# Merging three matrix products of a slot, splitting a norm over slots, and taking square roots on another engine

## The chip, the cores and the metric

The kernel runs on one core of a Trainium2 chip. A core has a matrix engine (TensorE, PE in the profile, with PEld for its weight loads), a vector engine (VectorE, DVE), an engine for activation functions (ScalarE, ACT), a general engine (GpSimd, POOL) and an engine that issues DMAs (SyncE, SP). Each works through its own queue in order; they wait for each other through semaphores. The metric is the time of one execution in microseconds (us); lower is better. Before the change it was 1166.24 us, the median of three runs (1165.88 to 1167.61).

## What is computed

The reference is a small perceiver of two layers over 64 batches of 32 latent rows of 256 features, so 2048 rows:

```
x = x + L0_xattn(layernorm(x), ctx)      # cross attention
x = x + L0_attn(layernorm(x))            # self attention, changed here
x = x + L0_ffn(layernorm(x))             # 16 blocks, the best 4 per row
x = x + L1_xattn(...); x = x + L1_attn(...); x = x + L1_ffn(...)
```

The self attention of layer 0 norms its input a second time, makes 16 heads of queries of 128 features, and one key and one value that all heads share:

```
xn = layernorm(x) * g_norm
q = xn @ Wq                    # 16 heads x 128
k, v = split(xn @ Wkv)         # one head
q, k = l2norm(q), l2norm(k)    # times 4 each
attn = softmax(q @ k.T)        # over the 32 rows of a batch
out = layernorm((attn @ v) @ Wout) * g_out
```

The feed forward part behind it chooses 4 of 16 blocks for each row by a softmax over a small product (`Wr`), and multiplies the hidden values with the mask of the chosen blocks.

## The kernel before

All 2048 rows lie in SBUF as 16 tiles `xs[t]` of 128 rows (4 batches each); four tiles make a group `g`. The self attention is a loop over slots, `for t in range(NT + 1)` with NT = 16. In its pool the order of the work on PE, DVE, ACT and POOL is the order in which the program is written (`manual_schedule`), so each engine's queue can be read off the code. Work of tile t and tile t-1 is interleaved in slot t:

- `query_part(n)` (line 868): two of the 16 heads of queries for a pair of tiles, a product `qb`, copied out by ACT (876). It runs ten parts ahead, one in each of the places 0 to 3 of a slot.
- `similar(t)`: scores `Sb` (899), four products that each use 32 columns of TensorE, one for each batch; then the sums of the squared queries `ssb` (907), of the same form. ACT takes the square root `rqb` (916).
- `gather(t - 1)`: the contexts `avb` of the tile before (946), four products that each use 32 rows of TensorE. DVE copies two of them into `oTb` (951), ACT the other two (953).
- `scale(t)`: DVE's reciprocal of `rqb` (921) and the product with the scores (923). `power(t)`: the exponential on ACT (927).
- `square(t + 1)`: POOL squares the next tile's queries (887).
- `project(t - 1)`: 16 products `yb` with the output weights (959). `norm_stats` and `norm_out`: the norm of the result, with ACT's square root (971), DVE's `ynb` (983) and POOL's product and addition to `xs[t]` (984, 985).
- `share(t)`: the denominators `denb` (933), their reciprocal (935) and the product (936), which gives the weights that the next slot's `gather` reads.
- `rotate(t)` and `fetch(t + 1)`: POOL's preparation of the context for layer 1, with its DMAs on SP, and `write_pad(t)`, which clears a tile on DVE (135, 136) and sends it out.

Into these slots other work is placed by `at(slot, place, function)`; `place(z)` issues query part z (for z below 4) and then what was placed there, in the order of the `at` calls. The places that matter here:

- keys of group g: `keys_norm(g)` (the two norms in a row, with statistics on DVE, lines 172 and 173, and ACT's square roots, 163) in slot 3 for group 2 and slot 6 for group 3, place 5; `keys_turn` (transposes and copies) in slots 4 and 8, place 2; `keys_of` (products `kvp`, 364, copies and squares on ACT, scaling on DVE, 378 to 380) in slots 5 and 9, places 1 and 3; `turn_keys` (transposes `kTp`, 387, copied by DVE, 389) in slots 6 and 10, place 2.
- routing of group g: `choose_norm` in slot 4g+5, place 5; `choose_turn` (transposes `tpr`, 633, copied by ACT, 636) in slot 4g+6, place 1; `choose_blocks` and `choose_best` (a product, 646, and then up to 26 small DVE instructions, 653 to 683) in slots 4g+7 and 4g+8, place 5.
- at the end of slot 2 DVE fills some number tables (756 to 764).
- from slot 10 on, the feed forward part of group 0: its norm (`ln_group(0, "c")`, slot 10, place 5), transposes (slot 12), hidden products (slots 13 to 15).

The products of a slot share eight PSUM banks: one for the scores, four (tag `W`) that `ssb`, the denominators and the four `avb` take in turn, one for `yb`, and two (tag `mm`) for everything else. A product that reuses a bank waits until the engine that reads its former content is done. `rstd_of` has two forms: a square root on ACT with a reciprocal on DVE, or, with `power=True`, an addition and a power of -0.5 on POOL (157, 158).

Of the kernel before, what the change touches and what calls it, by code (L numbers as in the profile page):

```python
# [7 lines left out]
F32 = mybir.dt.float32  # L8
AF = mybir.ActivationFunctionType
ALU = mybir.AluOpType  # L10
# [3 lines left out]
P = 128  # L14
B, S, D = 64, 32, 256
NT = B * S // P
# [11 lines left out]
EPS = 1e-5  # L28
# [19 lines left out]
def perceiver_kernel(ctx: ExitStack, tc: tile.TileContext, a: dict, out: bass.AP):  # L48
    nc = tc.nc
# [19 lines left out]
    def sm(name, shape):  # L69
        return small.tile(shape, F32, tag=name.split("_")[0], name=name)  # L70
# [4 lines left out]
    xs = [x[:, :D] for x in xf]  # L75
# [69 lines left out]
    mhalf = const.tile([P, 4], F32, name="mhalf")  # L145
# [62 lines left out]
    def ln_group(g, name, twice=False, act=False, power=False, sign=None):  # L208

        mv = sm(f"lnm_{name}{g}", [P, 4, 2])  # L210
        for i in range(4):
            stats(mv[:, i, :], xs[4 * g + i], f"{name}{g}_{i}", sign)
        rs, sh = ln_scale(mv, f"{name}{g}", twice, power)
        return [ln_out(xs[4 * g + i], rs, sh, i, f"{name}{g}", act) for i in range(4)]
# [127 lines left out]
    latT = {}  # L342
# [6 lines left out]
    def keys_norm(g):  # L349
        latT[g] = ln_group(g, "b", twice=True, act=True, power=g == 0)  # L350
# [273 lines left out]
    def choose_norm(g, act=True):  # L624
        choice[g] = ln_group(g, "r", act=act)

    def choose_turn(g, ps, work):
        xn = choice[g]
        xT = choice[g] = work.tile([P, KC, 512], F32, tag="xTr", name=f"xTr{g}", bufs=1)
        for k in range(KC):  # L630
            tp = ps.tile([P, 512], F32, tag="mm", name=f"tpr{g}_{k}")
            for i in range(4):
                nc.tensor.transpose(
                    tp[:, i * P : (i + 1) * P], xn[i][:, k * P : (k + 1) * P], ident
                )
            nc.scalar.copy(xT[:, k, :], tp)
        return xT
# [198 lines left out]
    with tc.tile_pool(name="wB", bufs=2) as work, tc.tile_pool(  # L836
# [167 lines left out]

        steps = {}

        def at(slot, place, fn):
            steps.setdefault((slot, place), []).append(fn)  # L1010

        for g in range(1, NG):
            at(4 * g - 4, 2, lambda g=g: keys_turn(g, ps2))
            slot, place_ = (0, 5) if g == 1 else (4 * g - 3, 1)
            at(slot, place_, lambda g=g: keys_of(g, ps2, 0))
            at(4 * g - 3, 3, lambda g=g: keys_of(g, ps2, 1))
            at(4 * g - 2, 2, lambda g=g: turn_keys(g, ps2))
            if g > 1:
                at((3, 6)[g - 2], 5, lambda g=g: keys_norm(g))
        for g in range(NG - 1):  # L1020
            at(4 * g + 5, 5, lambda g=g: choose_norm(g))
            at(4 * g + 6, 1, lambda g=g: choose_turn(g, ps2, work))
            at(4 * g + 7, 5, lambda g=g: choose_blocks(g, ps2, work))
            if g < NG - 2:
                at(4 * g + 7, 5, lambda g=g: choose_best(g, work, (0, 1)))
            at(4 * g + 8, 5, lambda g=g: choose_best(g, work, (2, 3)))
            if g < NG - 2:
                at(4 * g + 9, 2, lambda g=g: choose_store(g, ps2, work))
# [24 lines left out]

        at(10, 4, lambda: ff.update(mb=spread(0)))
        at(16, 2, lambda: ff.update(mb1=spread(1)))
        at(10, 5, lambda: ff.update(xn=ln_group(0, "c", act=True)))
        at(12, 2, ff_begin)
        for f, (slot, place) in enumerate(
            ((13, 2), (13, 3), (14, 0), (14, 1), (14, 2), (14, 3), (15, 0), (15, 1))
# [8 lines left out]
        for t in range(NT + 1):  # L1068


            parts = [AHEAD + 4 * t + z for z in range(4)]

            def place(z):
                if z < 4:
                    query_part(parts[z])
                for step in steps.get((t, z), ()):
                    step()

            if t < NT:
                similar(t)  # L1080
            place(0)
            if t > 0:
                gather(t - 1)
            if t < NT:
                scale(t)
            place(1)
            square(t + 1)
            ff_late()
            place(2)
            if t < NT:  # L1090
                power(t)
            ff_late()
            place(5)
            if t > 0:
                project(t - 1)
                norm_stats(t - 1)
            if t < NT:
                share(t)
            place(3)
            ff_late()  # L1100
            if t > 0:
                norm_out(t - 1)
            if t < NT:
                rotate(t, work)
            if t + 1 < NT:
                fetch(t + 1, work)
            place(4)
            if t == 2:
                numbers = all_numbers(counted)
                tri, one, token, base = (numbers[z] for z in ("tri", "one", "token", "base"))  # L1110
                ntile, n128e, n128h = (numbers[z] for z in ("ntile", "n128e", "n128h"))
            if t > 2:
                for t_ in {3: (0, 1), NT: (NT - 2, NT - 1)}.get(t, (t - 2,)):
                    nc.gpsimd.tensor_copy(xf[t_][:, D : D + 1], token[:, t_ : t_ + 1])
            write_pad(t)
            if t in (2, 4):
                load_c(t // 4)
# [1411 lines left out]
```

## Time and profile before

| | |
|---|---|
| median of three runs | 1166.24 us |
| profiled execution, its own time | 1165.13 us |
| its span, first to last instruction | 1163.4 us |
| TensorE's granted clock, mean | 0.988 |
| busy: PE, PEld | 1106.1, 788.6 us |
| busy: DVE, ACT, POOL | 769.4, 579.1, 455.9 us |
| the loop over slots | about 146 to 490 us of the span |

The page gives the busy time of each engine, the span in 40 slices, and the costliest groups of instructions. A line of a timeline gives the start, the length, the engine, the line of the program, the operation, the tile written and the tiles read, the shape and how many instructions were merged; in brackets, for how long the engine was idle before it and which engine ended that. A float32 matrix product counts as two instructions. A line of the table of stretches gives, after the bounds and the length, the busy time (and the number of instructions) of PE, PEld, DVE, ACT and POOL, the granted clock, the busy share of the DMA engines, and GB/s. A line of the list of waits says who waited for whom: the sum, how often, and the longest.

### The profile page before, as it was taken

Reading aid. Unit: us, or ns where it says so; the run is one execution under the profiler, and the core shown is the slowest. Engines: PE = TensorE matmul, PEld = TensorE weight load, DVE = VectorE, ACT = ScalarE, POOL = GpSimd, SP = SyncE. Lnnn points to the kernel's source line nnn. Section 1 sums busy time; section 2 is a strip of 40 time slices with the busy share of each in tenths; the row PEclk is TensorE's granted clock in tenths of the full one; section 3 lists DMA queues with packets and bytes.
Section 4 is the critical chain, followed back from the end, with each engine's and each line's share of the span. In section 5 each row is a group of like instructions: output and inputs, shape, how many; then the busy total and the mean of one; then the engine's idle time right before and its main releaser. Section 6 shows DMA issues by size and latency. Waiting matters only on the chain. (4 is left out here: it accounts for less than half of the span.)

```text
span 1163.4 us, 26376 instructions
## 1 busy us (share of the span) xinstructions
PE 1106.1 (95%) x10026; PEld 788.6 (68%) x10026; DVE 769.4 (66%) x1810; ACT 579.1 (50%) x1446; POOL 455.9 (39%) x766
## 2 busy tenths in 40 slices
PE   8999999899999999999998999999999988889997
PEld 5666766677767657667676777777776656555663
DVE  4886146868987987655225787777878566675532
ACT  3446363545455364231326777777777545442221
POOL 2443265777768787410001121121222356632111
PEclk9999999999999999999999999999999999999999
DMA  5221132546346446491213121212110175112413
GB/s 138 70 77 38 33 87 82 169 124 169 96 129 205 115 121 188 144 281 60 74 47 57 29 55 29 56 28 56 38 46 2 35 223 184 49 34 74 152 37 119
DMA packets 98990, 109.05 MB, mean 94 GB/s; under 512 B 37240, under 2 KB 73465, under 8 KB 98642
## 3 DMA queue, kind: packets, MB, share of 16 engines
q1 hardware_dynamic: 97138, 103.05, 31.2%
q0 software_dynamic: 1728, 4.33, 1.0%
q8 instruction: 80, 1.31, 0.5%
q14 instruction: 44, 0.36, 0.1%
HBM read 76.36 MB, written 31.41 MB: 93 GB/s over the span
## 5 line engine op out<-in xcount | busy, mean ns | idle before, releaser
L1441 ACT ACTIVATE pp<-Sd,nm 128x256 f32<-128x256 f32 x256 | 119.6, 480 | 39.9 <-POOL nm L1438 39.9
L868 PE MATMUL qb<-xT_b,b_q 128*128 128x256 f32 x512 | 122.3, 386 | 0.4 <-ACT qTb L876 0.4
L868 PEld LDWEIGHTS qb<-xT_b,b_q 128*128 128x128 f32 x512 | 94.7, 190 | 39.6 <-issue 19.3
L959 PE MATMUL yb<-b_o,oTb 128*128 128x256 f32 x512 | 115.2, 383 | 0.6 <-DVE oTb L951 0.5
L1437 DVE TENSOR_REDUCE nm<-Sd 128x2 f32<-128x512 f32 x128 | 79.4, 682 | 54.7 <-PE Sd L1424 54.7
L1438 POOL TENSOR_SCALAR nm<-nm 128x2 f32<-128x2 f32 x128 | 26.9, 210 | 222.9 <-DVE nm L1437 222.6
L959 PEld LDWEIGHTS yb<-b_o,oTb 128*128 128x128 f32 x512 | 97.3, 192 | 15.1 <-issue 1.6
L1459 DVE TENSOR_TENSOR pp<-pp,rd 128x512 f32<-128x512 f32 x128 | 89.5, 699 | 4.4
L1475 ACT COPY pTd<-pt 128x512 f32<-128x512 f32 x128 | 68.8, 590 | 10.5 <-PE pt L1469 4.8
L1469 PE MATMUL pt<-cst,pp 128*128 128x128 f32 x512 | 67.9, 274 | 5.9 <-DVE pp L1459 4.9
L887 POOL TENSOR_TENSOR q2b<-qTb 128x512 f32<-128x512 f32 x64 | 64.7, 1041 | 13.9 <-ACT qTb L876 13.9
L1469 PEld LDWEIGHTS pt<-cst,pp 128*128 128x128 f32 x512 | 59.1, 141 | 15.4 <-ACT ld L1449 4.9
L876 ACT COPY qTb<-qb 128x512 f32<-128x512 f32 x64 | 37.3, 584 | 63.7 <-PE qb L868 60.9
L1236 PE MATMUL qd<-xT_d,d_m 128*128 128x256 f32 x256 | 64.1, 394 | 0.7 <-DVE rd L1458 0.3
L921 DVE RECIPROCAL rqb<-rqb 128x512 f32<-128x512 f32 x16 | 53.5, 3342 | 17.1 <-ACT rqb L916 17.1
L1516 PE MATMUL yd<-d_n,co 128*128 128x256 f32 x256 | 63.2, 391 | 0.0
L1424 PE MATMUL Sd<-ct,qTd 64*128 64x256 f32 x480 | 60.0, 388 | 0.0
L1450 POOL TENSOR_TENSOR sd<-sd,ld 128x2 f32<-128x2 f32 x128 | 26.3, 206 | 85.8 <-ACT ld L1449 85.8
L722 PE MATMUL yc<-c,hc 128*128 128x256 f32 x256 | 58.5, 382 | 0.0
L1490 PE MATMUL od<-pTd,na 128*64 128x256 f32 x480 | 58.4, 385 | 0.0
L1516 PEld LDWEIGHTS yd<-d_n,co 128*128 128x128 f32 x256 | 46.2, 189 | 16.7 <-DVE nm L1437 7.7
L935 DVE RECIPROCAL rdb<-denb 128x512 f32<-128x512 f32 x16 | 53.6, 3353 | 5.8 <-PE denb L933 5.6
(424 smaller groups left out, 2417.6 us busy)
## 6 DMA issues: line engine op xcount, KB each, us to landing
srt<-pad SPq DMA_DIRECT2D x17, 1040.0 KB
mb<-maskd SPq DMA_DIRECT2D x64, 128.0 KB
ct<-ctd SPq DMA_DIRECT2D x30, 257.0 KB
rct<-in_ctxT_dram SPq DMA_DIRECT2D x32, 128.5 KB
rrt<-in_ctxT_dram SPq DMA_DIRECT2D x64, 64.2 KB
ctd<-rct SPq DMA_DIRECT2D x32, 128.5 KB
nad<-rna SPq DMA_DIRECT2D x16, 256.0 KB
fw<-in_f_wg_dram SPq DMA_DIRECT2D x16, 256.0 KB
```

Source lines behind the costliest of these rows:

```text
L722: nc.tensor.matmul(y_ps, hs[f][:, i * P : (i + 1) * P], c_2[:, f, :], start=(f == 0), stop=(f == 7),)
L868: nc.tensor.matmul(q_ps[:, hh, :], b_q[:, k, h * P : (h + 1) * P], xT[:, k, c0 : c0 + 256], start=(k == 0), stop=(k == KC - 1),)
L887: nc.gpsimd.tensor_tensor(q2[:, 4 * h4 : 4 * h4 + 4, :], q, q, ALU.mult)
L959: nc.tensor.matmul(y_ps, oT[:, h, :], b_o[:, h, :], start=(h == 0), stop=(h == NH - 1))
L1236: nc.tensor.matmul(q_ps[:, r, :], m[:, k, pr * P : (pr + 1) * P], xT[:, k, c0 : c0 + 256], start=(k == 0), stop=(k == KC - 1),)
L1424: nc.tensor.matmul(logits[b][hh][:, u, :], qT[hs, b % 8, 4 * u : 4 * u + 4, :], ct[hs, b % 4, :KEYS], start=True, stop=True,)
L1437: nc.vector.tensor_reduce(nm, s_ps[hh], AX.X, ALU.max, negate=True)
L1441: nc.scalar.activation(pb[:, u, hh, :], s_ps[hh][:, u, :], AF.Exp, bias=nm[:, u : u + 1], accum_out=sd[:, u : u + 1],)
L1459: nc.vector.tensor_tensor(pp, pp, bc(rd, 2, KEYS), ALU.mult)
L1469: nc.tensor.transpose(pts[c][:, hh * 256 + u * P : hh * 256 + u * P + P], probs[b][:, u, hh, c * P : (c + 1) * P], ident,)
L1475: nc.scalar.copy(pT[:, c, :], pt)
L1516: nc.tensor.matmul(y_ps, co[:, pr, :], n[:, pr, :], start=(pr == pr0), stop=(pr == pr0 + n_pr - 1),)
```

## The change

Three things change in the self attention of layer 0.

In slots 1 to 15 (`inner`), `similar(t)` moves behind `gather(t - 1)`, and query part 1, with what was placed there, moves ahead of `gather`. PE's queue then has two query blocks, the contexts, the scores and the squares in a row, where before it had scores, squares, a query block, contexts and a query block.

The keys' norm of groups 2 and 3 is written out in three steps in three slots (1, 2, 3 and 4, 5, 6): the statistics and a first power, then the second variance and a second power, then the product of the two and the normed rows.

The powers of these norms, of the routing's norms (groups 0 to 2) and of the norm of the feed forward part of group 0 are taken on POOL, with the shift too for the latter two; their normed rows are made on ACT at place 3 of the same slot (place 4 for group 2). The routing's transposes move from place 1 to place 2.

```diff
+        def norm_begin(g, name):
+            mv = sm(f"lnm_{name}{g}", [P, 4, 2])
+            for i in range(4):
+                stats(mv[:, i, :], xs[4 * g + i], f"{name}{g}_{i}")
+            rs = rstd_of(mv, 4, f"{name}{g}", True)
+            sh = sm(f"lnh_{name}{g}", [P, 4])
+            nc.gpsimd.tensor_tensor(sh, rs, mv[:, :, 0], ALU.mult)
+            nc.gpsimd.tensor_scalar(sh, sh, -1.0, None, ALU.mult)
+            begun[name, g] = rs, sh
+
+        def norm_end(g, name):
+            rs, sh = begun.pop((name, g))
+            return [ln_out(xs[4 * g + i], rs, sh, i, f"{name}{g}", True) for i in range(4)]
+
+        def keys_norm_step(g, z):
+            if z == 0:
+                mv = work.tile([P, 4, 2], F32, name=f"kbm_{g}", bufs=1)
+                for i in range(4):
+                    stats(mv[:, i, :], xs[4 * g + i], f"b{g}_{i}")
+                r1 = work.tile([P, 4], F32, name=f"kbr_{g}", bufs=1)
+                nc.gpsimd.tensor_scalar(r1, mv[:, :, 1], EPS, None, ALU.add)
+                nc.gpsimd.tensor_tensor(r1, r1, mhalf[:, 0:4], ALU.pow)
+                begun["b", g] = mv, r1
+            elif z == 1:
+                mv, r1 = begun["b", g]
+                r2 = work.tile([P, 4], F32, name=f"kbq_{g}", bufs=1)
+                nc.vector.tensor_tensor(r2, mv[:, :, 1], r1, ALU.mult)
+                nc.vector.tensor_tensor(r2, r2, r1, ALU.mult)
+                nc.gpsimd.tensor_scalar(r2, r2, EPS, None, ALU.add)
+                nc.gpsimd.tensor_tensor(r2, r2, mhalf[:, 0:4], ALU.pow)
+                begun["b", g] = mv, r1, r2
+            else:
+                mv, r1, r2 = begun.pop(("b", g))
+                nc.vector.tensor_tensor(r2, r2, r1, ALU.mult)
+                nc.vector.scalar_tensor_tensor(r1, mv[:, :, 0], -1.0, r2, ALU.mult, ALU.mult)
+                latT[g] = [ln_out(xs[4 * g + i], r2, r1, i, f"b{g}", True) for i in range(4)]
...
             if g > 1:
-                at((3, 6)[g - 2], 5, lambda g=g: keys_norm(g))
+                for z in range(3):
+                    at((1, 4)[g - 2] + z, 5, lambda g=g, z=z: keys_norm_step(g, z))
         for g in range(NG - 1):
-            at(4 * g + 5, 5, lambda g=g: choose_norm(g))
-            at(4 * g + 6, 1, lambda g=g: choose_turn(g, ps2, work))
+            at(4 * g + 5, 5, lambda g=g: norm_begin(g, "r"))
+            at(4 * g + 5, 3 + g // 2, lambda g=g: choice.update({g: norm_end(g, "r")}))
+            at(4 * g + 6, 2, lambda g=g: choose_turn(g, ps2, work))
...
-        at(10, 5, lambda: ff.update(xn=ln_group(0, "c", act=True)))
+        at(10, 5, lambda: norm_begin(0, "c"))
+        at(10, 3, lambda: ff.update(xn=norm_end(0, "c")))
...
-            if t < NT:
+            inner = 0 < t < NT
+            if t == 0:
                 similar(t)
             place(0)
+            if inner:
+                place(1)
             if t > 0:
                 gather(t - 1)
+            if inner:
+                similar(t)
             if t < NT:
                 scale(t)
-            place(1)
+            if not inner:
+                place(1)
             square(t + 1)
```

More of the change, by code (lines that the diff above doesn't have):

```diff
@@ L1002, in perceiver_kernel @@
                 square(0, (n_ // 2,))
+        begun = {}
+        def norm_begin(g, name):
[32 more added lines that the diff above has]
+                latT[g] = [ln_out(xs[4 * g + i], r2, r1, i, f"b{g}", True) for i in range(4)]
         steps = {}
```

## The prediction

> **What bounds the kernel now.** I read the page first (busy times, slices), then the busy table cut at every context product of layer 0's self attention, then the timelines of PE and DVE in single slots, then PE's list of waits. A slot is one turn of the loop over the 16 tiles; slot 7 is the one whose context product starts at 285.06.
>
> ```profile
> PE 1106.1 (95%) x10026; PEld 788.6 (68%) x10026; DVE 769.4 (66%) x1810; ACT 579.1 (50%) x1446; POOL 455.9 (39%) x766
> ```
>
> PE is the bound over the whole span. What counts in the changed stretch is PE's idle time and what it pays for switching shapes. The next table holds periods from one context product to the next (slots 3, 7, 8, 11, 12, 13); the idle time is the period less PE's busy time:
>
> ```profile
> 202.88:223.85 20.97, 18.30 (x91) 13.02 (x90) 19.89 (x40) 10.12 (x18) 14.84 (x15) 1.00 0.49 133
> 285.06:306.59 21.53, 19.85 (x108) 14.89 (x107) 19.38 (x31) 8.13 (x13) 15.28 (x16) 1.00 0.43 121
> 306.59:326.21 19.62, 19.29 (x98) 13.81 (x98) 18.80 (x27) 8.13 (x12) 15.43 (x16) 1.00 0.40 115
> 368.12:389.21 21.09, 19.85 (x108) 14.89 (x107) 18.82 (x29) 8.12 (x13) 14.84 (x16) 1.00 0.56 165
> 389.21:408.83 19.62, 19.29 (x99) 13.81 (x99) 18.80 (x27) 7.93 (x12) 15.43 (x16) 1.00 0.40 116
> 408.83:428.96 20.13, 18.87 (x84) 11.00 (x83) 17.75 (x30) 14.48 (x20) 16.88 (x18) 1.00 0.45 124
> ```
>
> The reader is to see that in slots 3, 7, 8, 11 and 12 DVE (third figure) is busy 18.8 to 19.9 us: there it is nearly a second bound. PE's list of waits names the same places:
>
> ```profile
> PE avb L946 <- DVE pTb L936: 5.1, 3, 2.2
> PE ssb L907 <- POOL q2b L887: 1.2, 2, 1.0
> PE yb L959 <- DVE oTb L951: 0.5, 1, 0.5
> ```
>
> The 5.1 us are 2.16 at the end of slot 3 (keys' norm of group 2 on DVE), 1.68 after slot 7 and 1.24 after slot 11 (routing choices on DVE). PE's order in an undisturbed slot:
>
> ```profile
> 362.52 1.89 PE L868 MATMUL qb<-xT_b,b_q 128*128 128x256 f32 x8
> 364.34 1.07 PE L899 MATMUL Sb<-qTb,kTb 128*32 128x512 f32 x8
> 365.22 1.04 PE L907 MATMUL ssb<-q2b,ones 128*32 128x512 f32 x8
> 366.19 1.99 PE L868 MATMUL qb<-xT_b,b_q 128*128 128x256 f32 x8
> 368.12 1.14 PE L946 MATMUL avb<-pTb,kvb 32*128 32x512 f32 x8
> 369.19 3.72 PE L868 MATMUL qb<-xT_b,b_q 128*128 128x256 f32 x16
> 372.75 0.52 PE L646 MATMUL lpc<-c_r,xTr 128*128 128x16 f32 x4
> ```
>
> The starts show the price of a switch: a query block between its like takes 1.73 (340.85 to 342.58), before S 1.82, between ss and av 1.93; two of them after av take 3.56, not 3.46; av lasts 1.07 and S 0.88 to the next start.
>
> **The change, part by part.** Sums are made against the profiled execution (span 1163.4, time 1165.13, 1.1 under the median of 1166.24).
>
> *1. One switch a slot.* The seven steps above take 10.23 (362.52 to 372.75). In the new order (q, q, q, av, S, ss, q) they take 1.73+1.73+1.83, then av and S, then 0.97+1.83. Av to S is not in the trace: between 0.88 (like S to ss) and 1.07 (like av to q), so 9.85 to 10.04, a saving of 0.19 to 0.38. But the new order takes PSUM buffers of the tag W in another sequence: ss now reuses the buffer of the first context product and so waits for DVE's first oT copy. That copy starts 1.16 after av (368.12, 369.28), lasts 0.69, and a wait of PE on DVE ends 0.06 after it (L936 ends 223.79, av starts 223.85): ss cannot start before av+1.91, which caps the saving at 0.23. I take 0.19, the value with av like its own row, in 12 of 15 slots (the other three are bound by DVE, item 4): -2.3; ends 0 (a bubble of 0.2 at each such wait) and -2.8.
>
> The trace has only av to q (1.07) and S to ss (0.88) for the missing step. [...] No row here shows that step.
>
> *2. The new wait of ss where DVE is late.* At the end of slot 2 DVE builds the number tables, ahead of the oT copies of slot 3:
>
> ```profile
> 200.95 0.69 DVE L936 TENSOR_TENSOR pTb<-pTb,rdb 128x512 f32<-128x512 f32 x1
> 203.95 1.30 DVE L758 TENSOR_SCALAR tri<-tri 128x128 f32<-128x128 f32 x1
> 206.75 0.69 DVE L951 COPY oTb<-avb 128x512 f32<-128x512 f32 x1
> ```
>
> The order stays. The first copy ends at 207.44; ss would be ready 1.95 after an av at about 202.6, so at 204.55. PE stalls 2.95 in front of ss, with the query block, the output projection and the sqrt of ss queued behind it. Before, two query blocks covered this and 0.51 was left. Net +2.44 (+2.0 to +3.0, by when av starts).
>
> *3. Keys' norm in three steps, powers on GpSimd.* In slot 3, DVE's 7.0 us from 211.94 to 218.98 (8 statistics instructions, two rounds of sqrt over ACT, 16 in all) become two tiny ones; the statistics move to slots 1 and 4, which have 6 us of DVE waiting for yb (5.31 and 6.64 at 176.39 and 236.92). The 2.16 go: -2.16, both ends. Slot 6 likewise, where nothing waited. POOL gets 24 tiny instructions (L158 power 1.04 and L157 add 0.23 elsewhere in the trace, so 1.3 a step and some 3.0 at most, in slot 5); they stand after the squares, where POOL waits 2.0 to 6.5 us for ynb in each slot: 0. No DMA is added; rotate and its DMAs stay behind ynb. ACT's normalised rows move behind the keys' copies, where POOL is done 1 us earlier (261.6 against 262.7, slot 5): 0; if that cover went, the query copy behind it would be late, and it has 3 us.
>
> *4. DVE's chain is longer.* ACT's sqrt starts 1.11 after ss starts and takes 0.69; the reciprocal now starts at av+3.85 (1.95+1.11+0.69+0.1), before at av+2.36 (285.06, 287.42): +1.49 in every slot. Where DVE has slack (R, the end of share's product, comes 5.1 after the denominator starts, the next av at 6.14) this costs nothing; the exponent is ready 5.9 after ss ends, the denominator comes 8.8 after. In slots 7, 8, 11 and 12 it has none. Slots 8 and 12: choices from 312.94 to 321.25, all under POOL's work (until 323.24), so they only shift; R comes at av+20.95, PE is ready at 19.4. After slot 12 that is 19.62 to 21.1: +1.48 (+0.5 to +2). After slot 8 the two keys' products (1.8) that place 1 brings ahead of av in slot 9 fill the gap: 19.4+1.8 against 21.1, so 0 (to +1.0). Slots 7 and 11: POOL ends 300.81, av+15.75, while the choices run. Beside POOL one costs up to 1.31, alone 0.22:
>
> ```profile
> 317.90 1.31 DVE L673 TENSOR_TENSOR eqc<-eqc,cst 128x64 f32<-128x64 f32 x1
> 469.11 0.22 DVE L673 TENSOR_TENSOR eqc<-eqc,cst 128x64 f32<-128x64 f32 x1
> ```
>
> Shifted by 1.49, two slowed ones (0.75 and 0.99) fall after POOL's end and become 0.26 each: 1.2 back, so +0.32 and +0.36 (each 0 to +1.5).
>
> *5. ss no longer waits for squares.* It comes 3.7 later in the slot: the delays of 0.39 (slot 5), 0.27 (9) and 1.2 (14, listed with 1.02) go: -1.86, both ends; slot 13's 0.27 is inside item 4.
>
> *6. The routing transposes in place 2.* In slots 6 and 10 they follow a query block and the keys' transpose, which holds one of the two buffers until DVE copies it, late. So each waits for an ACT copy: 0.45, then 0.9 between the two, 2.27 in all where 351.16 to 352.49 was 1.33: +0.94 each, +1.88 (+1.0 to +2.4). Slot 14 already had 0.71 of this: 0.
>
> Sum: -2.3 +2.44 -2.16 +1.48 +0.68 -1.86 +1.88 = +0.16, so 1166.4 from the median. Less than 0.2% (2.3 us) is about what a measurement of this kernel can't tell from no change. I forecast no change.
>
> **The rivals.** (A) Faster: DVE does not bind. If the shifted choices run so much more beside an idle POOL that slots 7, 8, 11 and 12 no longer hold PE, items of +2.16 go and the 1.68 and 1.24 too: 0.2-2.2-2.9 = -4.9, 1161.3; halfway, 1163.9. For it: 0.22 against 1.31. Against it: in slots 8 and 12 POOL outlasts the choices by 2 us even now. (B) Slower: DVE becomes the bound of those slots. If nothing is given back, each of slots 7 and 11 pays 1.49 (+2.3 over my sum), slot 9's cover fails (+1), and the wait of ss costs a bubble that eats item 1 (+2.3): 1172.0, half of it 1169.2. For it: 18.8 to 19.9 us busy of 19.6 to 21.5. It decides from 2.2 us above my sum on. (C) The change does not do what it says: the stall of 2.16 after slot 3 stays, because the late ss of that slot makes DVE late again: +2.16, 1168.6. Against it: 16 instructions less on DVE there.
>
> **How the numbers follow.** My forecast 0.42, A 0.25, B 0.25, C 0.08. C lies on the edge and is counted as slower: faster 0.25, same 0.42, slower 0.33. The likeliest one's own range is 1164.0 to 1168.5. The range over all reaches towards the ends of A and B: 1161.8 to 1171.2, some 0.1 left out on each side.
>
> **What would show it.** Right: the stall before av after slot 3 is gone, one of about 3 us stands before ss in slot 3, stalls before av of 2 to 2.3 after slots 7 and 11 and a new one near 1.7 after slot 12, none after slot 8; transposes of slots 6 and 10 spread over 2.2; undisturbed slots 0.2 shorter. Wrong: undisturbed slots shorter by 0.4 or not at all, or choices on DVE that take quite another time than 10.1 and 8.3 us.

## The result and the profile after

The changed kernel takes 1174.31 us (median of 6 runs, 1170.45 to 1176.46); the kernel before took 1165.95 us beside it (6 runs, 1162.51 to 1167.61). The ratio is 1.0067, 95% interval 1.0044 to 1.0090: slower by 0.67%, where no change was forecast, and outside the range given. The profiled execution took 1174.07 us, with a span of 1172.3 and a mean granted clock of 0.985.

The busy line of the page after (engine, us, share of the span, instructions):

```profile
PE 1106.8 (94%) x10026; PEld 790.9 (67%) x10026; DVE 758.8 (65%) x1790; ACT 575.8 (49%) x1437; POOL 469.4 (40%) x790
```

PE is as busy as before (1106.1) and DVE 10.6 us less; POOL does 13.5 us more. So the loss is PE's idle time. In what follows av, S, ss and q are short for the products `avb` (contexts), `Sb` (scores), `ssb` (sums of squares) and `qb` (a query block). The busy table cut at the context products, slots 3, 7, 8, 11, 12, 13 and 14 (columns as in the prediction: PE, PEld, DVE, ACT, POOL, granted clock, DMA share, GB/s):

```profile
204.23:225.13 20.90, 18.01 (x92) 13.15 (x91) 16.75 (x28) 9.58 (x15) 15.34 (x16) 1.00 0.47 130
286.33:308.09 21.76, 19.99 (x108) 14.84 (x107) 18.20 (x31) 8.13 (x13) 15.25 (x16) 1.00 0.41 118
308.09:330.07 21.98, 21.02 (x106) 15.31 (x106) 19.60 (x28) 9.34 (x16) 15.44 (x16) 1.00 0.42 114
370.71:392.53 21.82, 19.98 (x107) 14.83 (x106) 18.20 (x31) 8.13 (x13) 15.24 (x16) 1.00 0.56 164
392.53:414.14 21.61, 19.30 (x99) 13.87 (x99) 19.34 (x27) 8.37 (x13) 15.44 (x16) 1.00 0.41 116
414.14:432.30 18.16, 18.16 (x79) 10.38 (x79) 15.12 (x24) 8.92 (x11) 16.77 (x18) 1.00 0.41 120
432.30:456.86 24.56, 20.61 (x83) 11.57 (x82) 15.05 (x20) 14.68 (x21) 18.07 (x19) 0.93 0.52 160
```

The last line stands out: slot 14 takes 24.56, with 3.95 us in which PE is idle and, alone in this table, a granted clock under 1.00. PE's list of waits for the stretch from 145 to 500 us names what it idles for (total us, times, longest):

```profile
PE avb L946 <- DVE pTb L936: 3.9, 3, 1.4
PE ssb L907 <- DVE oTb L951: 2.9, 1, 2.9
PE hp L707 <- ACT xTr L636: 2.8, 1, 2.8
PE qb L868 <- ACT qTb L876: 2.5, 4, 0.7
PE tpr L633 <- ACT xTr L636: 1.4, 2, 0.7
PE tpr L633 <- ACT hc L714: 1.2, 1, 1.2
```

The first two were forecast. The third and the sixth, 4.0 us together, are slot 14's transposes and the hidden products behind them; the fourth is query blocks that wait for an ACT copy. The undisturbed slot, for the price of the merge (PE's timeline):

```profile
365.43 5.34 PE L868 MATMUL qb<-xT_b,b_q 128*128 128x256 f32 x24
370.71 1.14 PE L946 MATMUL avb<-pTb,kvb 32*128 32x512 f32 x8
371.78 1.06 PE L899 MATMUL Sb<-qTb,kTb 128*32 128x512 f32 x8
372.70 1.06 PE L907 MATMUL ssb<-q2b,ones 128*32 128x512 f32 x8
373.70 1.99 PE L868 MATMUL qb<-xT_b,b_q 128*128 128x256 f32 x8
375.53 1.63 PE L646 MATMUL lpc<-c_r,xTr 128*128 128x16 f32 x14
```

From 365.43 to 375.53 it is 10.10, before it was 10.23.

For a ledger that the clock of other stages does not touch, I count each slot from the start of its predecessor's denominator product (`denb`) to the start of its own, and the whole stretch from slot 0's denominators to the start of the output projection of slot 16. The stretch is 321.53 before and 327.96 after, +6.43. By slot (after less before, us; the forecast is the prediction's items put into their slots):

| slot | forecast | measured |
|---|---|---|
| 1, 2, 7, 11, 15 | -0.19 each | -0.14, -0.12, -0.13, -0.13, -0.14 |
| 3 | +2.25 | +2.16 |
| 4 | -2.35 | -2.37 |
| 5 | -0.58 | -0.54 |
| 6 | +0.75 | +0.66 |
| 8 | +0.32 | +0.23 |
| 9 | -0.46 | +0.56 |
| 10 | +0.75 | +0.66 |
| 12 | +0.36 | +0.74 |
| 13 | +1.48 | +1.37 |
| 14 | -1.39 | +3.60 |
| sum | +0.2 | +6.4 |

Slot 14 alone misses by 4.99, slot 9 by 1.02, slot 12 by 0.38, all others together by -0.2.

Slot 14's cause can be followed through three timelines of the changed kernel. POOL:

```profile
427.21 4.03 POOL L887 TENSOR_TENSOR q2b<-qTb 128x512 f32<-128x512 f32 x4
431.33 0.54 POOL L157 TENSOR_SCALAR lnr_r<-lnm_r 128x4 f32<-128x4 f32 x1
431.96 1.33 POOL L158 TENSOR_TENSOR lnr_r<-lnr_r,mhalf 128x4 f32<-128x4 f32 x1
...
433.66 0.24 POOL L1016 TENSOR_SCALAR lnh_r<-lnh_r 128x4 f32<-128x4 f32 x1
```

ACT:

```profile
428.97 0.60 ACT L714 ACTIVATE hc<-hp 128x512 f32<-128x512 f32 x1 [0.20 <-PE hp L707]
433.94 2.07 ACT L194 ACTIVATE xn_r<-x,lnh_r,lnr_r 128x256 f32<-128x256 f32 x4 [4.37 <-POOL lnh_r L1016]
435.91 1.06 ACT L714 ACTIVATE hc<-hp 128x512 f32<-128x512 f32 x2
436.87 1.06 ACT L953 COPY oTb<-avb 128x512 f32<-128x512 f32 x2
437.94 1.28 ACT L916 ACT_TABLE_LOAD   x1
439.24 0.69 ACT L916 ACTIVATE rqb<-ssb,qeps 128x512 f32<-128x512 f32 x1
439.82 1.06 ACT L636 COPY xTr<-tpr 128x512 f32<-128x512 f32 x2
```

PE:

```profile
434.29 1.07 PE L907 MATMUL ssb<-q2b,ones 128*32 128x512 f32 x8
436.54 1.14 PE L633 MATMUL tpr<-cst,xn_r 128*128 128x128 f32 x8 [1.18 <-ACT hc L714]
440.45 3.57 PE L707 MATMUL hp<-xT_c,c 128*128 128x512 f32 x4 [2.77 <-ACT xTr L636]
443.86 7.07 PE L959 MATMUL yb<-b_o,oTb 128*128 128x256 f32 x32
```

The granted clock behind these stalls, from 440 to 445 us:

```profile
440.00:445.00 5.00, 4.55 (x10) 2.53 (x11) 4.89 (x4) 3.09 (x5) 4.76 (x6) 0.66 0.92 305
```

In the kernel before, ACT began the same rows 0.63 after slot 13's denominators (421.30), not 7.75 after (426.19), behind a wait of 1.13 for DVE, and PE's wait for the copies of the transposes was 0.71 (ACT, then PE):

```profile
421.93 2.07 ACT L194 ACTIVATE xn_r<-x,lnh_r,lnr_r 128x256 f32<-128x256 f32 x4 [1.13 <-DVE lnh_r L187]
431.83 3.70 PE L707 MATMUL hp<-xT_c,c 128*128 128x512 f32 x8 [0.71 <-ACT xTr L636]
```

The reader is to see a queue that waits for a queue. DVE's last statistics instruction of this norm runs from 425.26 to 425.44, but POOL takes the statistics up behind four squares of slot 13, at 431.33, and needs 2.6 us. ACT's normed rows wait 4.37 for it, and two gelus, two copies, a square root and the copies of the transposes stand behind them. PE waits 1.18 and 2.77, and then the hidden product takes 3.41 to the next start where 1.77 was usual (two of them took 3.54 before): the granted clock is 0.66 behind the stall. The three add up to 1.18 + 2.06 (2.77 less the 0.71 of before) + 1.64 = 4.88 of the 4.99; 1.64 of that is the clock, the rest idle time.

### The profile page after: what moved, and what is told of

Read it like the earlier page. It is cut to its first block, busy times and chain, and to the rows that moved or that the text cites. A ratio compares the mean times of both kernels' runs of the same rounds, so it can differ in the third digit from the quotient of the medians.

```text
span 1172.3 us, 26414 instructions
## 1 busy us (share of the span) xinstructions
PE 1106.8 (94%) x10026; PEld 790.9 (67%) x10026; DVE 758.8 (65%) x1790; ACT 575.8 (49%) x1437; POOL 469.4 (40%) x790
## 5 line engine op out<-in xcount | busy, mean ns | idle before, releaser
L868 PE MATMUL qb<-xT_b,b_q 128*128 128x256 f32 x512 | 119.3, 384 | 2.8 <-ACT qTb L876 2.8
L887 POOL TENSOR_TENSOR q2b<-qTb 128x512 f32<-128x512 f32 x64 | 65.1, 1047 | 10.6 <-ACT qTb L876 10.6
```

Of the source, the lines that this page charges most:

```text
L868: nc.tensor.matmul(q_ps[:, hh, :], b_q[:, k, h * P : (h + 1) * P], xT[:, k, c0 : c0 + 256], start=(k == 0), stop=(k == KC - 1),)
L887: nc.gpsimd.tensor_tensor(q2[:, 4 * h4 : 4 * h4 + 4, :], q, q, ALU.mult)
```

## The experiments

Theory after the result: the rows of group 2 come late (POOL's powers behind the squares, ACT's queue behind the rows). Rival 1: place 2 as such costs slot 14, by PSUM buffers. Rival 2: the merge costs, by DVE's longer chain. Each ratio is against the kernel before, timed beside it on the same chip.

### 1. Group 2's routing norm back on DVE

```diff
-            at(4 * g + 5, 5, lambda g=g: norm_begin(g, "r"))
-            at(4 * g + 5, 3 + g // 2, lambda g=g: choice.update({g: norm_end(g, "r")}))
+            if g == 2:
+                at(13, 5, lambda: choose_norm(2))
+            else:
+                at(4 * g + 5, 5, lambda g=g: norm_begin(g, "r"))
+                at(4 * g + 5, 3, lambda g=g: choice.update({g: norm_end(g, "r")}))
```

> The changed kernel, with only the routing norm of group 2 (slot 13) put back on DVE and ACT's square root as before. The stretch is counted from the start of the first denominator product to the start of slot 16's output projection: 321.53 us before, 327.96 after; of the 6.43 between them 3.60 lie in slot 14 alone, from denominator to denominator 20.97 before and 24.57 after. Theory (late rows): GpSimd makes this group's factors only behind its four squares, at 433.9, ACT's normalised rows stand in front of two gelus and wait 4.37 for it, and all that follows on ACT and PE is late. Then slot 14 takes 20.2 to 21, the stretch 323.5 to 324.5, and the kernel is 0.3% slower than before, not 0.7%. Rival 1 (buffers: in place 2 the transposes of slot 14 compete with the hidden products for two PSUM buffers, whenever the rows come): slot 14 stays at 24 or more, the time unchanged from after. Rival 2 (the merge alone makes DVE's chain late): likewise unchanged.

Measured: slot 14 takes 20.61, the stretch 323.98; every other slot is within 0.02 of after. The transposes, in the same place 2, do not wait, and the product behind them waits 0.77 (PE's timeline):

```profile
435.57 1.09 PE L633 MATMUL tpr<-cst,xn_r 128*128 128x128 f32 x8
437.43 1.98 PE L707 MATMUL hp<-xT_c,c 128*128 128x512 f32 x4 [0.77 <-ACT xTr L636]
```

So 3.96 of the loss go with the late factors; rival 1 falls, and so does rival 2 for this slot. Slot 14 is still 1.03 over the forecast (19.58): the two waits here are the 0.77 and one of 0.66 in which a hidden product waits for a gelu, in front of which ACT's rows stand in this kernel too (426.53 to 428.61). But the time did not follow the stretch: ratio 1.0058 (1.0038 to 1.0078), 1170.08 us, where the stretch alone would give 1.002, and the expectation was a loss of 0.3%. That is taken up in runs 11 and 13.

### 2. Factors on POOL, but nobody behind the late rows

```diff
-            at(4 * g + 5, 3 + g // 2, lambda g=g: choice.update({g: norm_end(g, "r")}))
-            at(4 * g + 6, 2, lambda g=g: choose_turn(g, ps2, work))
+            slot, place_ = (14, 5) if g == 2 else (4 * g + 5, 3)
+            at(slot, place_, lambda g=g: choice.update({g: norm_end(g, "r")}))
+            at(4 * g + 6, 3 if g == 2 else 2, lambda g=g: choose_turn(g, ps2, work))
```

> The changed kernel, with the factors of group 2 still on GpSimd, but its rows on ACT moved from place 4 of slot 13 to place 5 of slot 14 (behind the gelus and the square root) and its transposes from place 2 to place 3 of slot 14. Theory (late rows hold ACT's queue): the factors come as late as after, but nobody needs them yet, so slot 14 takes 20.2 to 21.5 and the stretch 323.5 to 325. Rival 1 (buffers): the transposes still stand between hidden products, slot 14 takes 23 or more. Rival 2 (the powers as such are dear, by holding GpSimd's queue in front of the rotation): slot 14 near 24.5 and slot 15 late as well.

Measured: slot 14 takes 17.82 and slot 15, into whose count the transposes now fall, 19.27; the stretch is 322.73, the ratio 1.0043 (1.0027 to 1.0059). Slot 14 and the stretch lie below what was expected of the theory (20.2 to 21.5, 323.5 to 325). ACT's rows come behind slot 14's gelus, and the hidden product does not wait (ACT, then PE):

```profile
441.45 2.06 ACT L194 ACTIVATE xn_r<-x,lnh_r,lnr_r 128x256 f32<-128x256 f32 x4
435.36 1.98 PE L707 MATMUL hp<-xT_c,c 128*128 128x512 f32 x4
```

The powers stand in POOL's queue where they stood after, behind the four squares of slot 13, and cost nothing once ACT's rows are not in front of the gelus. Slots 14 and 15 together take 37.09, 5.37 less than after and 1.41 less than in experiment 1. The transposes had to move with the rows, from place 2 to place 3, so up to 1.41 may be the work of that move (in slots 10 and 11 of experiment 6 it is worth 0.79); with the transposes in place 2, experiment 1 shows the other 3.96.

### 3. The merge alone

```diff
-                for z in range(3):
-                    at((1, 4)[g - 2] + z, 5, lambda g=g, z=z: keys_norm_step(g, z))
+                at((3, 6)[g - 2], 5, lambda g=g: keys_norm(g))
...
-            at(4 * g + 5, 5, lambda g=g: norm_begin(g, "r"))
-            at(4 * g + 5, 3 + g // 2, lambda g=g: choice.update({g: norm_end(g, "r")}))
+            at(4 * g + 5, 5, lambda g=g: choose_norm(g))
...
-        at(10, 5, lambda: norm_begin(0, "c"))
-        at(10, 3, lambda: ff.update(xn=norm_end(0, "c")))
+        at(10, 5, lambda: ff.update(xn=ln_group(0, "c", act=True)))
```

> The changed order of contexts, scores and squares and place 2 for the transposes, with all norms as before (keys' norm in one piece on DVE in slots 3 and 6, the routing and expert norms on DVE and ACT). Theory (late rows are 4.8 of the loss, the merge is about even): stretch 321.5 to 326 with the stall of 2.2 or more back at the end of slot 3, slot 14 at 20 to 21. Rival 2 (the merge is what costs): stretch 327 or more, 0.5% slower than before or worse.

Measured: stretch 327.47 (+5.94), ratio 1.0043 (1.0026 to 1.0060). Slot 14 takes 20.62, as the theory has it; but slot 3 takes 23.73, against 20.90 after, and slot 4 19.20 without a stall. So the stretch is in rival 2's range: the merge by itself loses, in slot 3, and not in slot 14. The stall of 2.2 that was expected back at the end of slot 3, since the keys' norm is in one piece again, did not come: the contexts of slot 4 start at 228.26, without a wait. PE is late there by the stall in front of ss and by what follows. Slot 3 is odd. The stall is the same, but ss and the query block behind it are slower:

```profile
209.56 1.94 PE L907 MATMUL ssb<-q2b,ones 128*32 128x512 f32 x8 [2.90 <-DVE oTb L951]
211.43 3.78 PE L868 MATMUL qb<-xT_b,b_q 128*128 128x256 f32 x8
```

In the changed kernel the same three numbers are 2.89, 1.07 and 2.00. The busy table of the merge-only kernel shows why, in its column of the granted clock:

```profile
210.00:215.00 5.00, 5.00 (x16) 2.86 (x9) 2.74 (x2) 0.69 (x1) 4.76 (x6) 0.50 0.78 251
```

### 4. The norms alone

```diff
-            inner = 0 < t < NT
-            if t == 0:
+            if t < NT:
                 similar(t)
             place(0)
-            if inner:
-                place(1)
             if t > 0:
                 gather(t - 1)
-            if inner:
-                similar(t)
             if t < NT:
                 scale(t)
-            if not inner:
-                place(1)
+            place(1)
...
-            at(4 * g + 6, 2, lambda g=g: choose_turn(g, ps2, work))
+            at(4 * g + 6, 1, lambda g=g: choose_turn(g, ps2, work))
```

> The order of before and place 1 for the transposes, with the changed norms (keys' norm in three steps, powers on GpSimd). Theory (late rows): the stall of 2.16 at the end of slot 3 goes, but the rows of slot 14's transposes are 4 us late as after, and now needed earlier: slot 14 takes 24 or more, stretch 322 to 325, the kernel 0 to 0.3% slower than before. Rival 2 (the merge is what costs): stretch 319 to 320, 0.2% faster than before.

Measured: slot 4 takes 19.33 instead of 21.56 (-2.23: the keys' norm pays as forecast), slot 14 takes 27.67 instead of 20.97 (+6.70), all others are within 0.42 of before. Stretch 325.56, ratio 1.0035 (1.0018 to 1.0053). ACT's rows wait 4.01 for POOL here (4.37 after). PE's waits over 0.2 us in slot 14 add up to 4.28 (1.73 before, 3.95 after), and the two hidden products behind them take 5.88 to the next start, where 3.54 was usual, at a granted clock of 0.54 (435 to 440 us):

```profile
434.90 6.04 PE L707 MATMUL hp<-xT_c,c 128*128 128x512 f32 x8 [0.34 <-ACT xTr L636]
```

So some 2.3 of the 6.70 are the clock; that the late rows cost more in this order than with the merge is not shown. The merge alone (+5.94) and the norms alone (+4.03) make 9.97, together they make 6.43. The sum of the parts did not foretell it: low clock is in each (2.8 us of it in slot 3 of the merge alone), and slot 4's gain of 2.2 to 2.4 is in both.

### 5. The kernel before, once more

No edit.

> The kernel before, unchanged, once more. In all changed versions so far the first denominator product starts at 159.4 to 160.3, in the one profile of before at 158.1, though nothing ahead of it is changed. Theory (drift): the profile of before drew an early stage without a low granted clock, another execution starts at 159 to 161; stretch 321.4 to 321.7 again, ratio 0.998 to 1.002. Rival (the changed versions lose 1.3 to 2.2 us before the stretch, by code or data placed elsewhere): it starts at 158.1 again.

Measured: the first denominators start at 160.03, as after; the stretch is 321.34, the ratio 1.0005 (0.9993 to 1.0017). The same kernel, then, starts the stretch 1.94 apart in two executions; from 20 to 40 us the granted clock was 1.00 in the first and 0.91 in this one. What stands ahead of the stretch is such drift, not the change. By slot it repeats the profile of before within 0.02, but for slot 14 (20.76 against 20.97).

### 6. A tidier merge: number tables where DVE waits, transposes later

```diff
-            at(4 * g + 6, 2, lambda g=g: choose_turn(g, ps2, work))
+            at(4 * g + 6, 3 if g > 0 else 2, lambda g=g: choose_turn(g, ps2, work))
...
             place(5)
+            if t == 2:
+                numbers = all_numbers(counted)
...
             if t > 0:
                 project(t - 1)
```

(On top of experiment 2; the tables leave the end of slot 2.)

> The kernel of the second experiment (rows of group 2 late, its transposes in place 3), with the number tables moved from the end of slot 2 to the middle of slot 2 (after place 5, where DVE waits for the output projection), and slot 10's transposes in place 3. Theory (the stall in front of the squares' product in slot 3 is DVE's number tables, the 0.8 of slot 10 the place): slot 3 falls from 20.9 to 18.6 to 18.9, slot 10 from 22.33 to about 21.5, the stretch is 319 to 320.5, 1 to 2.5 less than before. Rival (the merge's gate on DVE's copy is late anyhow): slot 3 stays over 20, the stretch at 322 or more.

Measured: slot 3 takes 19.05, slot 10 20.11 and slot 11 21.08 (together 41.19 against 41.98 after), the stretch is 319.09, the ratio 0.9999 (0.9984 to 1.0014). Slot 3 came 0.15 over what was expected, since the tables make DVE 1.12 late for the context product instead (PE's timeline):

```profile
203.10 1.14 PE L946 MATMUL avb<-pTb,kvb 32*128 32x512 f32 x8 [1.12 <-DVE pTb L936]
204.17 1.07 PE L899 MATMUL Sb<-qTb,kTb 128*32 128x512 f32 x8
205.09 1.07 PE L907 MATMUL ssb<-q2b,ones 128*32 128x512 f32 x8
```

The stall in front of ss was the tables, as the prediction's step 2 has it; the rival falls.

### 7. The norms without the merge, and without a queue behind the late rows

```diff
-            at(4 * g + 6, 1, lambda g=g: choose_turn(g, ps2, work))
+            at(4 * g + 6, 3 if g == 2 else 1, lambda g=g: choose_turn(g, ps2, work))
...
+            slot, place_ = (14, 5) if g == 2 else (4 * g + 5, 3)
+            at(slot, place_, lambda g=g: choice.update({g: norm_end(g, "r")}))
```

(On top of experiment 4.)

> The order of before with the changed norms (the fourth experiment), and the rows of group 2 on ACT in place 5 of slot 14, its transposes in place 3. Theory (late rows are the whole loss of the norms): slot 14 falls from 27.67 to 18 to 21, slot 15 takes up to 1.5 more, the stretch is 317 to 320, 0.1 to 0.4% faster than before. Rival (powers on GpSimd cost more than the rows): the stretch stays at 322 or more.

Measured: slot 14 takes 19.18, slot 15 19.73, the stretch 319.00, the ratio 0.9977 (0.9960 to 0.9995). This kernel is faster than the one before and the changed one. With the rows out of the gelus' way nothing of the norms' loss is left (slots 14 and 15 take 38.91, before 39.00); the transposes moved here too, from place 1 to place 3.

### 8. A longer stall in slot 3

```diff
                 numbers = all_numbers(counted)
+                for _ in range(3):
+                    nc.vector.tensor_scalar(
+                        numbers["tri"], numbers["tri"], 0.0, None, ALU.is_gt
+                    )
```

> The changed kernel, with the comparison of the number tables (1.30 on DVE) done three times more at the end of slot 2, same values. The stall of PE in slot 3 gets 3.9 longer, from 2.9 to 6.8. In the merge-only run PE ran at a granted clock of 0.50 for some microseconds behind that stall, in the changed kernel's profile it did not, at the same 2.9. Theory (PE's idle time lowers the granted clock, at 2.9 only by chance, at 6.8 always): slot 3 takes 20.9 + 3.9 + about 1.7 = 26.5, with a low clock behind the stall. Rival (the low clock came by chance, whatever PE did): slot 3 takes 24.8.

Measured, in a single execution (1177.35 us, stretch 333.26): neither. The three comparisons took 2.54, not 3.9, and ss did not wait; the output projection behind it waited 3.13. In every other kernel with the merged order in slot 3 and the tables in front of it ss waited; why it does not here is not shown. Slot 3 takes 24.18. Without a stall it would take about 18.6 (before 18.74, less the merge's 0.13), so 2.4 are left beyond the 3.13 of idle time, and the clock is low there:

```profile
210.00:215.00 5.00, 2.95 (x7) 2.44 (x8) 4.94 (x8) 0.90 (x1) 4.76 (x6) 0.62 0.35 79
215.00:220.00 5.00, 5.00 (x17) 4.12 (x17) 2.47 (x4) 2.97 (x6) 4.58 (x5) 0.69 0.48 135
```

As to the clock that agrees with the theory, though the run did not make the stall that was meant. Slot 14, where nothing was edited, takes 26.00 here, against 24.57 after, with the same 1.19 and 2.77 of idle time and a granted clock of 0.50 from 445 to 450 us: a low clock behind one and the same stall can last longer.

### 9. Each order where it pays

```diff
-            inner = 0 < t < NT
-            if t == 0:
+            inner = t in (1, 2, 4, 5, 7, 10, 11, 14, 15)
+            if t < NT and not inner:
                 similar(t)
...
-            at(4 * g + 5, 3 + g // 2, lambda g=g: choice.update({g: norm_end(g, "r")}))
-            at(4 * g + 6, 2, lambda g=g: choose_turn(g, ps2, work))
+            slot, place_ = (14, 5) if g == 2 else (4 * g + 5, 3)
+            at(slot, place_, lambda g=g: choice.update({g: norm_end(g, "r")}))
+            at(4 * g + 6, (1, 3, 3)[g], lambda g=g: choose_turn(g, ps2, work))
```

> The changed norms with late rows for group 2, and the merged order only in slots 1, 2, 4, 5, 7, 10, 11, 14 and 15, the order of before in slots 3, 6, 8, 9, 12 and 13; transposes in place 1 of slot 6, place 3 of slots 10 and 14. Theory (each slot's price is its own: the merge gains 0.13 where DVE is not late, and loses 0.3 to 1.4 where it is): the slots add up from the sixth and seventh experiments, 315.5 to 317.5 for the stretch, 0.3 to 0.5% faster than before. Rival (a late DVE is only handed to the next slot): 318.5 to 320, no better than either.

Measured: ratio 0.9961 (0.9941 to 0.9982), the lowest of all, though its interval overlaps that of experiment 7; 1160.63 us against 1164.33 beside it. The stretch is 317.91, 0.4 over the theory's range and under the rival's. All slots but the eighth lie within 0.55 of the kernel that the sum took them from (slot 13 takes 19.26, as in the seventh experiment, not 20.60, as in the sixth, though slot 11 is merged: its late DVE is not handed on). Slot 8 takes 22.83 instead of 20.73, and it is the clock again (granted 0.69 from 310 to 315 us), behind a stall of 1.75:

```profile
308.19 1.14 PE L946 MATMUL avb<-pTb,kvb 32*128 32x512 f32 x8 [1.75 <-DVE pTb L936]
309.26 5.41 PE L868 MATMUL qb<-xT_b,b_q 128*128 128x256 f32 x16
```

Two query blocks take 3.72 in the seventh kernel's slot 8, behind a stall of 1.33; here 5.41.

### 10 to 12. Three kernels once more

No edits: the changed kernel, the first and the seventh experiment.

> The changed kernel, unchanged, once more. The stall of slot 14 (1.18 and 2.77) comes again; by the theory of the low clock behind a stall slot 14 takes 24.6 to 26, by chance 22.8, and slot 3 20.9, or 22 to 24 where the low clock falls there; stretch 326 to 331; ratio 1.0045 to 1.009 as on record.

Measured: ratio 1.0086 (1.0063 to 1.0109), stretch 329.70. Slot 14 takes 24.59, with 1.19 and 2.77 of idle time, where 22.8 was expected if the low clock behind them had been chance; slot 3 takes 22.54 at the same stall of 2.90, and this time the query block behind it takes 3.34:

```profile
206.03 1.36 PE L907 MATMUL ssb<-q2b,ones 128*32 128x512 f32 x8 [2.90 <-DVE oTb L951]
207.31 3.34 PE L868 MATMUL qb<-xT_b,b_q 128*128 128x256 f32 x8
```

> The kernel of the first experiment once more, beside the changed kernel on one chip. Its stretch of 323.98 is 2.45 above before, 0.2%, but its timed ratio was 1.0058 (1.0038 to 1.0078). Theory (the rest is drift of the clock in other stages, or a low clock behind the 2.9 stall of slot 3 in some executions, 2 to 3 us): ratio 1.001 to 1.005, below that of the changed kernel. Rival (something outside the stretch is slower in it): ratio 1.005 or more again.

Measured: slot 3 22.54, slot 14 20.62, stretch 325.63, ratio 1.0076 (1.0049 to 1.0104). The timed ratio is over 1.005 again, so the rival holds: this kernel is timed slower than its stretch makes it. Nothing in its profiles outside the stretch is slower than before (from the end of the stretch to the end of the span 680.4 and 684.5 us, before 683.8 and 680.6).

> The kernel of the seventh experiment once more, beside the mixed order. Stretch 319.0 again (18.7 for slot 3, 19.2 for slot 14); ratio 0.996 to 0.9995 by the theory that the changed norms pay once nothing waits for the late rows, 0.9995 to 1.001 by the rival that its first ratio was chance.

Measured: stretch 318.68, ratio 0.9978 (0.9953 to 1.0003). The same value as the first time, though this interval by itself just takes in no change.

### 13 and 14. Is the excess the stall of slot 3?

```diff
             place(5)
+            if t == 2:
+                numbers = all_numbers(counted)
...
```

(On top of experiment 1. Run 14 is the sixth kernel unchanged.)

> The kernel of the first experiment (group 2's norm on DVE), with the number tables moved to the middle of slot 2, as in the sixth. Slot 3 falls from 20.9 (22.54 in the second profile) to 19.05, the stretch to 322.1. Theory (the excess of the timed ratio is the stall of slot 3 and the low clock behind it): ratio 0.999 to 1.0025. Rival (the excess comes from elsewhere, whether the stall is there or not): 1.004 to 1.006.

Measured: slot 3 takes 19.04, the stretch is 322.11 as expected, the ratio 1.0035 (1.0021 to 1.0048). Without the stall the ratio is 0.23 to 0.41% lower, 2.7 to 4.8 us, of which the stretch shows 1.9 to 3.5 (its interval overlaps that of the first run of experiment 1, and lies under that of the second). But it lies between the two expectations: about 3.5 us remain for which the stretch (+0.58) has no place.

> The kernel of the sixth experiment once more: no long stall in slots 3 and 14, stretch 319.1, 2.4 less than before. Theory (as in the run beside it): ratio 0.9965 to 0.9995. Rival (an excess of 2 us or more in every merged kernel): 0.9995 to 1.002, as the first time.

Measured: stretch 319.14, ratio 0.9976 (0.9955 to 0.9996): no excess here, and in this run the kernel is faster than the one before. Its first ratio was 0.9999 with the same stretch, so between nothing and 0.24% is what the two runs say together.

What stays open is the excess of the first and thirteenth kernels, and of the second (1.0043, where the stretch gives 1.0010). In the three profiled executions of the first and thirteenth the time outside the stretch is that of before (839.8, 841.4 and 842.4 us, before 841.9 and 840.7); in that of the second it was 845.3. A low clock behind their shorter stalls in executions that were not profiled would be of the right size, but it was not seen.

All kernels at a glance (stretch against 321.53):

| kernel | stretch | ratio |
|---|---|---|
| after (1, and 10) | +6.43, +8.17 | 1.0067, 1.0086 |
| rows of group 2 by DVE (1, 11) | +2.45, +4.10 | 1.0058, 1.0076 |
| the same without slot 3's stall (13) | +0.58 | 1.0035 |
| rows late in ACT's queue (2) | +1.20 | 1.0043 |
| merge alone (3) | +5.94 | 1.0043 |
| norms alone (4) | +4.03 | 1.0035 |
| longer stall (8, one execution) | +11.73 | - |
| merge, rows late, tables moved (6, 14) | -2.44, -2.39 | 0.9999, 0.9976 |
| norms, rows late (7, 12) | -2.53, -2.85 | 0.9977, 0.9978 |
| mixed order, rows late (9) | -3.62 | 0.9961 |

## Why the prediction was wrong

**What failed: two zeros for one place.** Step 3 said that POOL's tiny instructions stand after the squares, where POOL waits in each slot, "0", and that ACT's rows move behind the keys' copies, where POOL is done earlier, "0". The first zero asked whether POOL has room, not when its result is needed; the cover of the second was read in slot 5 and taken for all. In slot 13 the order on POOL is the same, but POOL begins its four squares at 427.21 and ends the factors at 433.9, while DVE had handed over the statistics at 425.4; and what stands behind the rows on ACT there is not a query copy with 3 us to spare but gelus, which PE's next products wait for. Step 6 then said that slot 14 "already had 0.71 of this: 0". Together they were priced at nothing and cost 4.99 against the forecast for slot 14. Experiment 1 takes 3.96 of it away by the norm alone, experiment 2 all of it by the place of the rows and of the transposes that read them, with the norm still on POOL. Of the 4.99, 3.24 are idle time and 1.64 the low clock behind it.

**Step 2, right but not whole.** The stall in front of ss was forecast as 2.95 and is 2.89; slot 3 came out at +2.16 for +2.25. But a stall was priced as idle time alone. In three of the six profiles that have it (experiments 3, 10, 11), the clock behind it was low (granted 0.50 and 0.67 over five microseconds in experiments 3 and 10, 0.91 over the twenty from 200 us in experiment 11) and it cost 1.6 to 2.8 more; behind slot 14's stall it cost 1.6 in the changed kernel's profile. No length from which on a stall has this cost was shown: 2.90 us sufficed here three times, 2.89 and 2.90 in the other three profiles did not, 1.75 sufficed once (experiment 9), and a wait of 1.0 in slot 16 in eight profiles (last section).

**Step 1, a size.** The merge saves 0.13 in an undisturbed slot, not 0.19: av to S takes 1.07, the value taken (an estimate, since no row of the kernel before has that step), but S to ss takes 0.92 and ss to q 1.00, 0.03 to 0.04 more than before.

**Step 3's other half, step 5 and the first half of step 6, right.** The 2.16 at the end of slot 3 are gone (slot 4 -2.37). In the order of before the split norm does that (experiment 4, -2.23); in the merged order it is not shown that it is needed, since in experiment 3, with the norm in one piece, slot 4 takes 19.20 too, behind a slot 3 that the new stall and a low clock made late. The waits for POOL's squares are gone (slot 5 -0.54). Slots 6 and 10 pay +0.66 for +0.75.

**Step 4, half right.** Slot 8 pays +0.23 for +0.32 and slot 13 +1.37 for +1.48. Slot 9 was to be covered by the keys' products and pays +0.56 for -0.46; slot 12 pays 0.38 too much. In slot 12 the term is mis-sized: the choices of slot 11 take 8.98 us for 9.70 before, so 0.72 comes back of the 1.2 that was forecast (in slot 7 it is 8.98 for 10.13, 1.15 back). In slot 9 a term was missed, a query copy. ACT's square root of the output norm waits for DVE, and with the choices on DVE it ends late; the query block of place 1, which now comes ahead of the contexts, waits for the copy behind it. ACT, then PE, in slot 9 of the changed kernel:

```profile
325.61 0.20 ACT L971 ACTIVATE lns_bo<-lnv_bo 128x1 f32<-128x1 f32 x1 [7.24 <-DVE lnv_bo L969]
325.72 1.05 ACT L876 COPY qTb<-qb 128x512 f32<-128x512 f32 x2
```

```profile
326.34 2.00 PE L868 MATMUL qb<-xT_b,b_q 128*128 128x256 f32 x8 [0.72 <-ACT qTb L876]
```

It happens four times, in slots 8, 9, 12 and 13, 2.5 us in all in the list of waits. In slots 8, 12 and 13 av waits for DVE right behind it, so there it is covered, and those stalls are 1.29 to 1.36, not about 2. Only in slot 9 does PE then run on, at 330.07; without the 0.72 it would have waited there for DVE's product, which ends at 329.64, so the copy itself accounts for about 0.4 of slot 9's miss of 1.02. No experiment changed this wait by itself, so it is read from the timelines alone.

**The rivals.** B ended on the right side by luck: its mechanism (DVE binds slots 7, 8, 11 and 12) is worth about 1.4 beyond the sum here (slots 9 and 12), not 2.8 to 5.6, and slot 14 was not among its slots. C is out, the stall it spoke of is gone. A is out, the stalls before av in slots 8, 12 and 13 are there (1.29, 1.29 and 1.36).

## What to carry to other kernels

When a small piece of work moves to another engine, look at every slot in which it runs, not at one: what is ahead of it on the new engine there, and which instructions stand behind its consumer in that queue. A thing that comes late costs nothing until something urgent is queued behind its reader; moving the reader (experiment 2) can be worth as much as speeding up the writer. And an order that pays in a slot with slack can lose in one without: the version with the shortest stretch (experiment 9) chose by slot.

## What the hardware showed unexpectedly

Behind stalls of PE the granted clock fell to 0.50 to 0.78 over five microseconds, which cost 1.6 to about 3 us on top of the stall in slots 3, 8 and 14. The stall of 2.9 us in slot 3 did so in three of six profiles (slot 3: 20.89, 20.90 and 20.90 without, 22.54, 22.54 and 23.73 with it), the pair of 1.18 and 2.77 in slot 14 in all three that have it (1.6 to 1.7 us twice, 3.1 in experiment 8), one of 2.15 in experiment 4 and one of 1.75 in experiment 9; those of 1.3 in the changed kernel and the one of 2.16 and 2.17 in the two profiles of before did not. A wait of 1.0 us in slot 16 (with two of 0.16 behind it), which every version has, was followed by an output projection whose first 24 instructions took 6.51 to 7.13 us in eight of the sixteen profiles, both of the kernel before among them, and 5.45 in the other eight; the granted clock behind it was 0.66 over five microseconds in the first profile of before and in that of the changed kernel. So the length of a stall does not decide it by itself, and what does is not shown. In a forecast of this kernel such a stall needs a second, larger end: what those of slots 3 and 16 (2.9 and 1.0 us) cost changed from one execution to the next.
